# Attention with a routed mixture of experts on one core: weighed values turned by transposing transfers instead of by TensorE

## The chip, the cores and the metric

The kernel runs on one core of one Trainium2 chip. The time is the device time of one launch in microseconds. TensorE (PE) multiplies and transposes through PSUM, VectorE (DVE), ScalarE (ACT) and GpSimd (POOL) work on SBUF and PSUM, and each of them works through its own queue of instructions in order. Transfers are issued by an engine's queue (here mostly SyncE, called SP, and GpSimd) and are carried out by 16 DMA engines.

## What is computed

16 sequences of 256 tokens of width 256, float32. The result is x + attention(layernorm(x)) + experts(layernorm(x)).

```python
# attention: H = 16 heads of hd = 16
q = q * cos + rotate_half(q) * sin              # k likewise
scores = einsum('bhqd,bhkd->bhqk', q, k) / sqrt(16)
attn = softmax(where(causal, scores, lowest))
out = einsum('bhqk,bhkd->bhqd', attn, v)
# experts: E = 8, inner width I = 512
probs = softmax(x @ router_w.T)
w = top_p_weights(probs, 0.9)                   # kept probabilities, not renormalised
for e in range(8):
    out = out + (silu(x @ gate_w[e].T) * (x @ up_w[e].T)) @ down_w[e].T * w[:, e:e+1]
```

## The kernel before

**Tiles.** The 4096 tokens are 32 tiles of 128 (`xs`, resident in SBUF), two to a sequence. The 16 heads are four groups (`c`) of four heads. In PSUM there are two small buffers (`ps_m`) and three of two banks each (`ps_sc`).

**Attention stage (L772 to L900).** For each sequence there are eight steps, two (`p`) to a group of heads, so 128 steps. What a step does, in the order of the code:

- `products` (L657): scores with queries in the partitions (`s`) of this step, and scores with keys in the partitions (`st`) of the step 11 before (`LAG`). The two come in one burst of eight matmuls. Each takes one of the three `ps_sc` buffers.
- `probabilities`: masks added to `st` by matmuls (L694), then one exponential on ScalarE (L699, `pr`), which frees the buffer.
- `maxima` (L670): four VectorE reductions over `s`. They free its buffer. The maxima of a sequence (`top`) are transposed once per sequence by TensorE (`turn`, L682), copied by ScalarE and added to `qT` by GpSimd (L688), so that `st` comes out with its maximum already taken away.
- one job of `prep_jobs` for the next sequence: projections `pq` and `pv` (L525, L541) with their bias additions on VectorE (L530, L545), the copy of the router's `logits` (L551), the rotation of queries and keys (VectorE L560, L561, L563; GpSimd L564, L567), transposes of normalised rows, keys and queries (`xnt` L514, `kt` and `qt` L578), norms on ScalarE (L490), and stores of normalised rows as split 16-bit halves (`half`, L501, stored by SP at L504).
- two steps after every second `st`, `weigh` (L709): eight matmuls multiply the probabilities of four heads with their values and, in a 17th column, with ones. `o` is 128 rows (32 for each head) by 256 tokens. ScalarE copies it to SBUF (`oT`, L715).
- one step later, `finish`: TensorE transposes `oT` back (`ot`, L721, two matmuls into a small PSUM buffer), VectorE takes the reciprocals of the sums (`rs`, L724) and scales (`at`, L726), GpSimd adds to `xs` (L730). After a sequence's last group its two tiles of `xs` are stored to `out`, by SP's queue for the first 13 sequences and by GpSimd's for the last three (L736).
- every second sequence the router (L595 to L626), in pieces over steps: softmax, the comparison of each probability with the others, the kept weights `wts`, stored by SP (L626).

When the last step of `s` is made, the 11 `st` left are made two in a step. The code is written in the order of the program; a scheduler then decides the order in each engine's queue, within what `issue_after` and priorities demand.

**Dispatch.** `count` and `find_wave` (from L257) find, for each expert and each of its rows, which token belongs there. A wave covers up to three blocks of 128 rows for four experts. `fetch` gathers such rows (normalised row and weights) with an indirect DMA of GpSimd (L411).

**Expert stage (L903 to the end).** A list of items: for each expert four groups of up to three blocks. The last item (expert number `E`) is the overflow item of one block, for an expert that more than 1472 tokens chose. For each item: rows gathered two items ahead, turned by `turn_in` one item ahead (a transposing transfer of 16-bit halves on SP, L916, then a copy by VectorE or ScalarE that joins them, L922), `expand` (gate and up products L936, Silu L941, product L942), and one item later `contract`: the product with the third weight (L978), scaling on ScalarE (L985), and an indirect DMA of GpSimd that adds the rows to `out` (L1004). Before the overflow item GpSimd drains its queue (L1036). Waves 2 and 3 of the first four experts are searched in items 0 and 1 (L1015); an item that searches fetches its rows after that.

At the end stands a branch for an expert with more rows than the overflow item holds; it isn't taken.

Of the kernel before, what the change touches and what calls it, by code (L numbers as in the profile page):

```python
# [36 lines left out]
def kernel(  # L37
# [35 lines left out]
    xs = const.tile([P, NT, D], F32, name="xs")  # L73
    nc.sync.dma_start(xs[:, 0:2, :], xf[:, 0:2, :])

    wqkv_sb = const.tile([P, DC, 3 * D + E], F32, name="wqkv_sb")
    nc.sync.dma_start(wqkv_sb[:, :, : 3 * D], wqkv.rearrange("(c p) e -> p c e", p=P))
    nc.sync.dma_start(wqkv_sb[:, :, 3 * D :], wr.rearrange("(c p) e -> p c e", p=P))
# [3 lines left out]
    nc.sync.dma_start(rope_sb, rope.rearrange("(q p) t d -> p q t d", p=P))  # L82
    for t0, t1 in ((2, 4), (4, 8), (8, 16), (16, 24), (24, 32)):
        nc.sync.dma_start(xs[:, t0:t1, :], xf[:, t0:t1, :])
# [236 lines left out]
    def find(h, js, to, numbers, token, name, pool, tag):  # L321
# [4 lines left out]
        def judge(r):  # L326
            nc.vector.tensor_copy(part[:, r, :n, 0:2], seen[r][:, :n, P:])
            for i, j in enumerate(js):
                less = gat.tile([P, P], F32, tag="less", name=f"less_{name}", bufs=2)
# [112 lines left out]
    for e in range(E):  # L442
        work += [(e, js) for js in (GROUPS[-1:] + GROUPS[:-1] if e % 2 else GROUPS)]
    work += [(E, (NB - 1,))]
    AHEAD = 2
    fetched = {}

    with tc.tile_pool(name="prep", bufs=2) as prep, tc.tile_pool(
# [58 lines left out]

        def prep_xnT(b):

            xnT = seqs[b][3]  # L510
            tp = ps_m.tile([P, NQ, DC, P], F32, tag="m", name=f"xnt_{b}")
# [3 lines left out]
            ins = nc.scalar.copy(xnT.rearrange("p c (q t) -> p q c t", q=NQ), tp)  # L515
            if b < 2:
                scalar_last.append(ins.ins)
# [17 lines left out]
        def prep_v(b, qi):  # L535

            t = b * NQ + qi
            xnT = seqs[b][3]
            pv = ps_m.tile([P, D + E], F32, tag="m", name=f"pv_{t}")
            for c in range(DC):  # L540
                nc.tensor.matmul(  # L541
                    pv, xnT[:, c, ts(qi, P)], wqkv_sb[:, c, 2 * D :],
                    start=(c == 0), stop=(c == DC - 1),
                )
            nc.vector.tensor_tensor(  # L545
                va[b % 4][:, qi, :, :HD],
                pv[:, :D].rearrange("p (h d) -> p h d", h=H),
                bias[:, 2 * D :].rearrange("p (h d) -> p h d", h=H),
                ALU.add,
            )  # L550
            nc.vector.tensor_copy(logits[:, t, :], pv[:, D:])  # L551

# [75 lines left out]
        W = 3 * P  # L628

        def products(kinds):  # L630

# [11 lines left out]
            for first in (True, False):  # L643
                for left, right, c, p, sc, by_key in made:
                    if by_key:
                        to, lhs = (slice(2 * P, W), slice(P, S)) if first else (
                            slice(0, 2 * P), slice(0, P))
                    else:
                        to, lhs = (slice(0, P),) * 2 if first else (slice(P, W), slice(P, S))
                    for j in range(2):  # L650
                        rows = slice(32 * (2 * p + j), 32 * (2 * p + j) + 32)

                        with ExitStack() as hold:
                            if opened is not None:
                                hold.enter_context(tc.high_priority(offset=400))
                                hold.enter_context(tc.issue_after(opened.ins))
                            opened = nc.tensor.matmul(  # L657
                                sc[:, j, to], left[rows, c, lhs],
                                right[rows, c, lhs if first else slice(0, S)],
                                start=first, stop=False, skip_group_check=True,  # L660
                            )
            return [m[4] for m in made]

        def maxima(b, c, p, sc):

            for j in range(2):
                for qi in range(NQ):
                    lo, hi = (0, P) if qi == 0 else (P, W)
                    junk = probs.tile([P, 2 * P], F32, tag="junk", name=f"junk_{b}", bufs=2)
                    ins = nc.vector.tensor_tensor_reduce(  # L670
# [6 lines left out]
        def turn(b):  # L677
# [7 lines left out]
            topT = probs.tile([P, S], F32, tag="topT", name=f"topT_{b}", bufs=2)  # L685
            nc.scalar.copy(topT, tp.rearrange("p q t -> p (q t)"))  # L686
# [3 lines left out]
        def probabilities(b, c, p, sc):  # L690

            for j in range(2):
                for k in (0, 2):
# [3 lines left out]
                    )  # L697
            pr = probs.tile([P, 2, W], F32, tag="pr", name=f"pr_{b}_{c}_{p}", bufs=6)
            scalar_last.append(nc.scalar.activation(pr, sc[:, :, :W], AF.Exp).ins)  # L699
            return pr  # L700

        def weigh(b, c, prs):
# [3 lines left out]
            for kc in range(NQ):  # L706
                for hh in range(4):
                    pr, j = prs[hh // 2], hh % 2
                    nc.tensor.matmul(  # L709
                        o[32 * hh : 32 * hh + 32, kc * P :], v[:, kc, 4 * c + hh, :],  # L710
                        pr[:, j, : 2 * P] if kc == 0 else pr[:, j, 2 * P :],
                        start=(kc == 0), stop=(kc == NQ - 1), skip_group_check=True,
                    )
            oT = probs.tile([P, S], F32, tag="oT", name=f"oT_{b}_{c}", bufs=2)
            nc.scalar.copy(oT, o)  # L715
            return oT

        def finish(b, c, oT):
            ot = ps_m.tile([P, NQ, P], F32, tag="m", name=f"ot_{b}_{c}")
            for qi in range(NQ):  # L720
                nc.tensor.transpose(ot[:, qi, :], oT[:, ts(qi, P)], ident)  # L721
            ot = ot.rearrange("p q (h d) -> p (q h) d", d=HP)
            rs = probs.tile([P, NQ * 4], F32, tag="rs", name=f"rs_{b}_{c}", bufs=2)
# [9 lines left out]
            if c == CH - 1:  # L733
                tiles = slice(b * NQ, (b + 1) * NQ)

                queue = nc.sync if b < B - 3 else nc.gpsimd  # L736
                queue.dma_start(of[:, tiles, :], xs[:, tiles, :])
            return ins.ins
# [89 lines left out]
        while late < len(steps) or weighed or finished:  # L828
# [73 lines left out]

    with tc.tile_pool(name="hid", bufs=2) as hid:  # L903

        def open_in(k):
            return hid.tile([P, DC, 3 * P], F32, tag="xT", name=f"xT_{k}")

        turned = {}

        def turn_in(xT, i, xg, name, p0=0, p1=P, pair=None):  # L910
# [3 lines left out]
            if p0 == 0:  # L914
                half = hid.tile([P, 2 * DC, P], U16, tag="half", name=f"xt_{name}_{i}", bufs=6)
# [6 lines left out]
            (nc.scalar.copy if i % 2 else nc.vector.tensor_copy)(  # L922
                both[:, :, :, i * P : i * P + n],
# [90 lines left out]

        waves = {0: [(0, 2)], 1: [(0, 3)]}  # L1015
        for w in range(len(WAVES) - 1):
# [4 lines left out]

        with tc.issue_after(freed[-3]), tc.issue_after(scalar_last[-1]):
            for q in range(len(work[0][1])):
                turn_in(xT[0], q, fetched[0][q][0], 0)
        for i in range(len(work) + 1):
# [14 lines left out]
            if i == 2 * len(GROUPS) - 1:  # L1040
                at_once(count(1))
            searched = chain(*(find_wave(*wave, ps_sc, "sc") for wave in waves.get(i, ())))
            if i == 3 * len(GROUPS) + 2:
# [103 lines left out]
```

## Time and profile before

| | us |
|---|---|
| median of 3 runs | 901.17 (900.65 to 902.33) |
| the profiled execution | 904.55 |
| its span, first to last instruction | 902.8 |
| mean granted TensorE clock in it | 0.991 |

The profile is of one execution. In the table below each row is a group of instructions of one line: how many, their busy time in all and the mean of one.

| line, engine | what | count | busy us | mean ns |
|---|---|---|---|---|
| L936, L978 PE | products of the experts | 1792 | 537.8 | 380 to 481 |
| L657 PE | scores, both kinds | 2048 | 239.2 | 348 and 355 |
| L670 DVE | maxima | 512 | 151.7 | 351 |
| L699 ACT | exponentials | 128 | 103.5 | 811 |
| L1004 POOL | adding rows to `out` | 96 | 150.8 | 1571 |
| L411 POOL | gathering rows | 92 | 97.0 | 1054 |

Matmuls are pipelined, so that the busy times of a group's instructions overlap; how long something holds TensorE is read from start to start. The span in 40 equal slices, with the busy share of each slice in tenths (9 is 90% or more), shows the two stages:

```profile
DVE  3898888878787879743121245432121212111210
ACT  2476565556555555442222222222222222222221
```

VectorE and ScalarE are used heavily in the attention stage, the first 17 slices or so, and lightly in the expert stage.

### The profile page before, as it was taken

The numbers are of one execution on the slowest core, as the hardware profiler recorded it, in microseconds if no ns is written. First come the engines' busy times: TensorE is split into PE (matmuls) and PEld (weight loads), VectorE is DVE, ScalarE is ACT, GpSimd is POOL, SyncE is SP. The second block draws the span as 40 slices with busy tenths as digits, with TensorE's granted clock in tenths as the row PEclk, the third lists the DMA queues.
The fourth block names the chain that finished last, engine by engine and source line by source line (L and its number), as shares of the span: only waits on it lengthen the run. The fifth ranks groups of instructions, "written<-read, shape, count | busy, mean of one in ns | idle before, by whom it ended". The sixth has DMA issues, their size and how long they took to land. (4 is left out here: it accounts for less than half of the span.)

```text
span 902.8 us, 17259 instructions
## 1 busy us (share of the span) xinstructions
PE 875.5 (97%) x6394; PEld 587.8 (65%) x6394; DVE 442.3 (49%) x2067; ACT 349.3 (39%) x644; POOL 404.4 (45%) x475
## 2 busy tenths in 40 slices
PE   7999999999999999989999999999999999999995
PEld 4556666666666666646676666766667766667674
DVE  3898888878787879743121245432121212111210
ACT  2476565556555555442222222222222222222221
POOL 6334333333333332424555545545554464556433
PEclk9999999999999999999999999999999999999998
DMA  7107100000000020134775463565665655656332
GB/s 240 36 8 244 31 25 26 25 26 26 25 26 26 25 95 20 32 78 80 116 134 96 74 146 65 95 103 107 116 103 82 123 99 114 108 82 121 54 36 33
DMA packets 96573, 69.98 MB, mean 78 GB/s; under 512 B 59840, under 2 KB 87616, under 8 KB 96480
## 3 DMA queue, kind: packets, MB, share of 16 engines
q0 software_dynamic: 19792, 30.86, 20.9%
q1 hardware_dynamic: 76688, 37.94, 16.5%
q8 instruction: 52, 0.85, 0.4%
q14 instruction: 41, 0.34, 0.1%
HBM read 32.14 MB, written 24.43 MB: 63 GB/s over the span
## 5 line engine op out<-in xcount | busy, mean ns | idle before, releaser
L1004 POOL DMA_INDIRECT out<-ys,tokens x96 | 150.8, 1571 | 205.4 <-ACT ys L985 188.3
L942 DVE TENSOR_TENSOR hT<-act,gu 128x384 f32<-128x384 f32 (+2 forms) x132 | 69.4, 526 | 258.0 <-ACT act L941 257.8
L936 PE MATMUL gu<-xT,wg 128*128 128x384 f32 (+1 forms) x512 | 183.6, 481 | 3.7 <-ACT oT L715 2.9
L936 PE MATMUL gu<-xT,wu 128*128 128x384 f32 (+1 forms) x512 | 179.8, 474 | 0.0
L978 PE MATMUL py<-wd,hT 128*128 128x256 f32 (+1 forms) x768 | 174.4, 380 | 1.9 <-DVE hT L942 1.9
L978 PEld LDWEIGHTS py<-wd,hT 128*128 128x128 f32 (+1 forms) x768 | 137.7, 186 | 40.2 <-DVE hT L942 2.3
L670 DVE CUSTOM_DVE_ANT_0 junk<-s,mask 128x128 f32<-128x128 f32 (+1 forms) x512 | 151.7, 351 | 17.2 <-PE s L657 15.9
L941 ACT ACTIVATE act<-gu 128x384 f32<-128x384 f32 (+2 forms) x132 | 62.2, 471 | 243.1 <-PE gu L936 243.1
L699 ACT ACTIVATE pr<-st 128x768 f32<-128x768 f32 x128 | 103.5, 811 | 102.2 <-PE st L694 100.0
L936 PEld LDWEIGHTS gu<-xT,wu 128*128 128x128 f32 x512 | 97.9, 191 | 61.9 <-issue 1.7
L936 PEld LDWEIGHTS gu<-xT,wg 128*128 128x128 f32 x512 | 96.7, 192 | 48.9 <-ACT oT L715 3.2
L657 PE MATMUL st<-qT,kT 32*128 32x128 f32 (+1 forms) x1024 | 120.6, 355 | 0.5 <-POOL qT L688 0.5
L657 PE MATMUL s<-kT,qT 32*128 32x128 f32 (+1 forms) x1024 | 118.6, 348 | 2.1 <-ACT pr L699 1.3
L411 POOL DMA_INDIRECT xg<-rows,tokens x92 | 97.0, 1054 | 37.3 <-issue 25.9
L730 POOL TENSOR_TENSOR xs<-xs,at 128x128 f32<-128x128 f32 x64 | 30.1, 471 | 140.2 <-DVE at L726 139.0
L985 ACT ACTIVATE ys<-py,xg 128x256 f32<-128x256 f32 (+1 forms) x96 | 45.4, 473 | 115.8 <-PE py L978 114.4
L657 PEld LDWEIGHTS st<-qT,kT 32*128 32x128 f32 x1024 | 68.7, 184 | 22.1 <-issue 16.9
L922 DVE COPY xT<-xt 128x512 uint16<-128x512 uint16 x65 | 25.9, 442 | 99.7 <-PE gu L936 84.5
L657 PEld LDWEIGHTS s<-kT,qT 32*128 32x128 f32 x1024 | 67.4, 185 | 7.2 <-issue 3.0
L525 PE MATMUL pq<-wqkv_sb,xnT 128*128 128x512 f32 x128 | 63.8, 622 | 3.6 <-DVE qk L530 2.2
L688 POOL TENSOR_TENSOR qT<-qT,topT 128x256 f32<-128x256 f32 x64 | 50.8, 826 | 22.2 <-ACT topT L686 22.2
L564 POOL TENSOR_TENSOR kp<-qk,rot 128x256 f32<-128x256 f32 x32 | 23.2, 726 | 77.3 <-DVE rs L724 42.5
(162 smaller groups left out, 942.3 us busy)
## 6 DMA issues: line engine op xcount, KB each, us to landing
rows<-half SPq DMA_DIRECT2D x32, 128.0 KB, 1.7
wg<-in_wg SPq DMA_DIRECT2D x8, 512.0 KB, 4.0
wu<-in_wu SPq DMA_DIRECT2D x8, 512.0 KB, 6.3
wd<-in_wd SPq DMA_DIRECT2D x8, 512.0 KB, 3.9
out<-xs SPq DMA_DIRECT2D x13, 256.0 KB, 2.2
xs<-in_x SPq DMA_DIRECT2D x3, 1024.0 KB, 11.6
rows<-zeros POOLq DMA_DIRECT2D x1, 1716.0 KB, 8.7
out<-zeros POOLq DMA_DIRECT2D x1, 1664.0 KB, 13.3
```

The lines of the kernel that those rows point to most:

```text
L411: nc.gpsimd.indirect_dma_start(out=xg[:n, :], out_offset=None, in_=halves, in_offset=bass.IndirectOffsetOnAxis(ap=token, axis=0),)
L525: nc.tensor.matmul(pq, xnT[:, c, ts(qi, P)], wqkv_sb[:, c, : 2 * D], start=(c == 0), stop=(c == DC - 1),)
L657: opened = nc.tensor.matmul(sc[:, j, to], left[rows, c, lhs], right[rows, c, lhs if first else slice(0, S)], start=first, stop=False, skip ...
L670: ins = nc.vector.tensor_tensor_reduce(junk[:, : hi - lo], sc[:, j, lo:hi], mask[:, 2 * P - (hi - lo) :], -1.0, -MASKED, ALU.add, ALU.min, ...
L688: nc.gpsimd.tensor_tensor(qT[:, c, :], qT[:, c, :], topT, ALU.add)
L699: scalar_last.append(nc.scalar.activation(pr, sc[:, :, :W], AF.Exp).ins)
L936: nc.tensor.matmul(gu[:, j, :w], w_sb[:, c, ts(i, P)], xT[:, c, :w], start=(c == 0), stop=(c == DC - 1),)
L941: nc.scalar.activation(act[:, :w], gu[:, 0, :w], AF.Silu)
L942: nc.vector.tensor_tensor(hT[:, i, :w], act[:, :w], gu[:, 1, :w], ALU.mult)
L978: nc.tensor.matmul(py[p0:p1, :], hT[:, i, k * P : k * P + p1 - p0], expert_w[e][2][:, i, :], start=(i == 0), stop=(i == IC - 1), skip_grou ...
L985: nc.scalar.activation(ys[p0:p1, :], py[p0:p1, :], AF.Copy, scale=weights_of(e, xg, p0, p1))
L1004: ins = nc.gpsimd.indirect_dma_start(out=out, out_offset=bass.IndirectOffsetOnAxis(ap=to[:p1, :], axis=0), in_=ys[:p1, :], in_offset=None, ...
```

## The change

The main part is in `weigh` and `finish`. ScalarE now copies `o` to SBUF as two planes of 16-bit halves (the low and the high halves of each float32 number). A transposing transfer in SP's queue turns these 512 rows of 128 halves into `half`. GpSimd joins the halves to float32 numbers in SBUF (`ot`, 17 of each 32 columns). VectorE's reciprocal and its multiplication then read SBUF where they read PSUM before. TensorE no longer takes part, and no small PSUM buffer is used. In the code `finish` stands four steps after the weighing instead of one (two in the tail).

```diff
-            oT = probs.tile([P, S], F32, tag="oT", name=f"oT_{b}_{c}", bufs=2)
-            nc.scalar.copy(oT, o)
-            return oT
+            tensor_last.append(ins.ins)
+            oT = probs.tile([P, 2, S], U16, tag="oT", name=f"oT_{b}_{c}", bufs=3)
+            nc.scalar.copy(oT, o.bitcast(U16).rearrange("p (s h) -> p h s", h=2))
+            half = probs.tile([P, 2, NQ * 4, HP], U16, tag="oh", name=f"oh_{b}_{c}", bufs=3)
+            nc.sync.dma_start_transpose(
+                half.rearrange("p h (q g) d -> p (h q) (g d)", q=NQ),
+                oT.rearrange("p h s -> p (h s)"),
+            )
+            return half
...
-            ot = ps_m.tile([P, NQ, P], F32, tag="m", name=f"ot_{b}_{c}")
-            for qi in range(NQ):
-                nc.tensor.transpose(ot[:, qi, :], oT[:, ts(qi, P)], ident)
-            ot = ot.rearrange("p q (h d) -> p (q h) d", d=HP)
+            ot = probs.tile([P, NQ * 4, HD + 2], F32, tag="ot", name=f"ot_{b}_{c}", bufs=2)
+            both = ot.rearrange("p g d -> p (g d)").bitcast(U16)
+            both = both.rearrange("p (g d h) -> p h g d", g=NQ * 4, h=2)
+            nc.gpsimd.tensor_copy(both[:, :, :, : HD + 1], half[:, :, :, : HD + 1])
             rs = probs.tile([P, NQ * 4], F32, tag="rs", name=f"rs_{b}_{c}", bufs=2)
             nc.vector.reciprocal(rs, ot[:, :, HD])
...
-                queue = nc.sync if b < B - 3 else nc.gpsimd
-                queue.dma_start(of[:, tiles, :], xs[:, tiles, :])
+                nc.gpsimd.dma_start(of[:, tiles, :], xs[:, tiles, :])
...
-                    finished.setdefault(i + 3, []).append(k)
+                    finished.setdefault(i + (6 if i < len(steps) else 4), []).append(k)
```

All stores of rows to `out` are thereby issued by GpSimd. The other edits:

**Tail of the attention stage.** Where two `st` are made in a step, their burst may only be issued behind the last weighing so far.

```diff
+                            elif len(kinds) == 2 and kinds[1][1] and tensor_last:
+                                hold.enter_context(tc.issue_after(tensor_last[-1]))
```

**Buffers.** `less`, `junk` and `topT` have one buffer instead of two, `pr` five instead of six.

**Start.** The first two tiles of `xs` come in a transfer each. Of `wqkv` only the columns of queries and keys come ahead of the bias and the rotation's factors; those of the values and of the router come behind. The statistics, norms and transposes of sequence 0 are made tile by tile. Those of tiles 2 and 3 come behind the last `logits` copy of sequence 0.

```diff
-        for t in range(NQ):
-            sums_of(t)
-        statistics(0, NQ)
...
-        prep_norm(0)
-        prep_xnT(0)
-        for t in range(NQ, 2 * NQ):
-            sums_of(t)
-        statistics(NQ, NQ)
+        for qi in range(NQ):
+            sums_of(qi)
+            statistics(qi, 1)
+            prep_norm(0, (qi,))
+            prep_xnT(0, qi, 1)
         for qi in range(NQ):
             prep_qk(0, qi)
-            prep_v(0, qi)
+            ins = prep_v(0, qi)
             for _ in rotation():
                 pass
+        with tc.issue_after(ins.ins):
+            for t in range(NQ, 2 * NQ):
+                sums_of(t)
+            statistics(NQ, NQ)
```

**Into the experts.** The first three `turn_in` stand behind the fourth last addition to `xs` alone (before: behind the third last and the last exponential), their buffers come from a pool of their own (`rows_in`), and their copies are all made by VectorE. Both waves are searched in item 0, one before each of its second and third quarters.

```diff
-        waves = {0: [(0, 2)], 1: [(0, 3)]}
+        waves = {0: [(0, 2), (0, 3)]}
...
-        with tc.issue_after(freed[-3]), tc.issue_after(scalar_last[-1]):
+        with tc.issue_after(freed[-4]):
...
-                if q == 1 and i in waves:
-                    at_once(searched)
-                    if i + AHEAD < len(work):
+                if q > 0 and searches:
+                    at_once(searches.pop(0))
+                    if q == 1 and i + AHEAD < len(work):
                         fetched[i + AHEAD] = fetch(*work[i + AHEAD])
```

**End.** The overflow item stands ahead of the last item instead of behind it.

```diff
-    work += [(E, (NB - 1,))]
+    work.insert(len(work) - 1, (E, (NB - 1,)))
```

More of the change, by code (lines that the diff above doesn't have):

```diff
@@ L73 @@
     xs = const.tile([P, NT, D], F32, name="xs")
-    nc.sync.dma_start(xs[:, 0:2, :], xf[:, 0:2, :])
+    for t in range(2):
+        nc.sync.dma_start(xs[:, t : t + 1, :], xf[:, t : t + 1, :])
     wqkv_sb = const.tile([P, DC, 3 * D + E], F32, name="wqkv_sb")
-    nc.sync.dma_start(wqkv_sb[:, :, : 3 * D], wqkv.rearrange("(c p) e -> p c e", p=P))
-    nc.sync.dma_start(wqkv_sb[:, :, 3 * D :], wr.rearrange("(c p) e -> p c e", p=P))
+    wf = wqkv.rearrange("(c p) e -> p c e", p=P)
+    nc.sync.dma_start(wqkv_sb[:, :, : 2 * D], wf[:, :, : 2 * D])
     bias = const.tile([P, 3 * D], F32, name="bias")
@@ L82 @@
     nc.sync.dma_start(rope_sb, rope.rearrange("(q p) t d -> p q t d", p=P))
+    nc.sync.dma_start(wqkv_sb[:, :, 2 * D : 3 * D], wf[:, :, 2 * D :])
+    nc.sync.dma_start(wqkv_sb[:, :, 3 * D :], wr.rearrange("(c p) e -> p c e", p=P))
     for t0, t1 in ((2, 4), (4, 8), (8, 16), (16, 24), (24, 32)):
@@ L328, in judge @@
             for i, j in enumerate(js):
-                less = gat.tile([P, P], F32, tag="less", name=f"less_{name}", bufs=2)
+                less = gat.tile([P, P], F32, tag="less", name=f"less_{name}", bufs=1)
                 nc.vector.tensor_scalar(
@@ L506, in store, with prep_xnT @@
             )
-        def prep_xnT(b):
+        def prep_xnT(b, q0=0, n=NQ):
             xnT = seqs[b][3]
-            tp = ps_m.tile([P, NQ, DC, P], F32, tag="m", name=f"xnt_{b}")
+            tp = ps_m.tile([P, n, DC, P], F32, tag="m", name=f"xnt_{b}_{q0}")
             for qi, xn in enumerate(normed.pop(b)):
@@ L514, in prep_xnT @@
                     nc.tensor.transpose(tp[:, qi, c, :], xn[:, ts(c, P)], ident)
-            ins = nc.scalar.copy(xnT.rearrange("p c (q t) -> p q c t", q=NQ), tp)
+            ins = nc.scalar.copy(
+                xnT.rearrange("p c (q t) -> p q c t", q=NQ)[:, q0 : q0 + n], tp
+            )
             if b < 2:
@@ L550, in prep_v @@
             )
-            nc.vector.tensor_copy(logits[:, t, :], pv[:, D:])
+            return nc.vector.tensor_copy(logits[:, t, :], pv[:, D:])
         def rotation():
@@ L628 @@
         W = 3 * P
+        tensor_last = []
         def products(kinds):
@@ L668, in maxima @@
                     lo, hi = (0, P) if qi == 0 else (P, W)
-                    junk = probs.tile([P, 2 * P], F32, tag="junk", name=f"junk_{b}", bufs=2)
+                    junk = probs.tile([P, 2 * P], F32, tag="junk", name=f"junk_{b}", bufs=1)
                     ins = nc.vector.tensor_tensor_reduce(
@@ L684, in turn @@
                 )
-            topT = probs.tile([P, S], F32, tag="topT", name=f"topT_{b}", bufs=2)
+            topT = probs.tile([P, S], F32, tag="topT", name=f"topT_{b}", bufs=1)
             nc.scalar.copy(topT, tp.rearrange("p q t -> p (q t)"))
@@ L697, in probabilities @@
                     )
-            pr = probs.tile([P, 2, W], F32, tag="pr", name=f"pr_{b}_{c}_{p}", bufs=6)
+            pr = probs.tile([P, 2, W], F32, tag="pr", name=f"pr_{b}_{c}_{p}", bufs=5)
             scalar_last.append(nc.scalar.activation(pr, sc[:, :, :W], AF.Exp).ins)
@@ L708, in weigh @@
                     pr, j = prs[hh // 2], hh % 2
-                    nc.tensor.matmul(
+                    ins = nc.tensor.matmul(
                         o[32 * hh : 32 * hh + 32, kc * P :], v[:, kc, 4 * c + hh, :],
@@ L713, in weigh, with finish @@
                     )
-            oT = probs.tile([P, S], F32, tag="oT", name=f"oT_{b}_{c}", bufs=2)
-            nc.scalar.copy(oT, o)
-            return oT
-        def finish(b, c, oT):
-            ot = ps_m.tile([P, NQ, P], F32, tag="m", name=f"ot_{b}_{c}")
-            for qi in range(NQ):
-                nc.tensor.transpose(ot[:, qi, :], oT[:, ts(qi, P)], ident)
-            ot = ot.rearrange("p q (h d) -> p (q h) d", d=HP)
+            tensor_last.append(ins.ins)
[5 more added lines that the diff above has]
+                oT.rearrange("p h s -> p (h s)"),
+            )
+            return half
+        def finish(b, c, half):
+            ot = probs.tile([P, NQ * 4, HD + 2], F32, tag="ot", name=f"ot_{b}_{c}", bufs=2)
+            both = ot.rearrange("p g d -> p (g d)").bitcast(U16)
+            both = both.rearrange("p (g d h) -> p h g d", g=NQ * 4, h=2)
+            nc.gpsimd.tensor_copy(both[:, :, :, : HD + 1], half[:, :, :, : HD + 1])
             rs = probs.tile([P, NQ * 4], F32, tag="rs", name=f"rs_{b}_{c}", bufs=2)
@@ L900 @@
         at_once(todo)
-    with tc.tile_pool(name="hid", bufs=2) as hid:
+    with tc.tile_pool(name="rows_in", bufs=2) as rows_in, tc.tile_pool(
+        name="hid", bufs=2
+    ) as hid:
         def open_in(k):
-            return hid.tile([P, DC, 3 * P], F32, tag="xT", name=f"xT_{k}")
+            return rows_in.tile([P, DC, 3 * P], F32, tag="xT", name=f"xT_{k}")
         turned = {}
@@ L914, in turn_in @@
             if p0 == 0:
-                half = hid.tile([P, 2 * DC, P], U16, tag="half", name=f"xt_{name}_{i}", bufs=6)
+                half = rows_in.tile(
+                    [P, 2 * DC, P], U16, tag="half", name=f"xt_{name}_{i}", bufs=6
+                )
                 nc.sync.dma_start_transpose(half, xg[:, : 2 * D])
@@ L921, in turn_in @@
             both = both.rearrange("p (c t h) -> p h c t", c=DC, h=2)
-            (nc.scalar.copy if i % 2 else nc.vector.tensor_copy)(
+            (nc.scalar.copy if i % 2 and name else nc.vector.tensor_copy)(
                 both[:, :, :, i * P : i * P + n],
@@ L1041 @@
                 at_once(count(1))
-            searched = chain(*(find_wave(*wave, ps_sc, "sc") for wave in waves.get(i, ())))
+            searches = [find_wave(*wave, ps_sc, "sc") for wave in waves.get(i, ())]
             if i == 3 * len(GROUPS) + 2:
```

## The prediction, made before the changed kernel ran

> **What bounds it now.** First the busy shares and the table of stretches: in the attention stage (46 to 393 us of the span) and in the expert stage TensorE never rests for long, so what it does and what makes it wait is the time. Columns of the second fence: stretch, then length and busy time of TensorE, its weight loads, VectorE, ScalarE, GpSimd, then TensorE's granted clock and the DMA share.
>
> ```profile
> PE 875.5 (97%) x6394; PEld 587.8 (65%) x6394; DVE 442.3 (49%) x2067; ACT 349.3 (39%) x644; POOL 404.4 (45%) x475
> ```
> ```profile
> 84.00:107.00 23.00, 22.68 (x272) 14.30 (x271) 21.33 (x108) 14.82 (x27) 8.14 (x12) 1.00 0.36 114
> ...
> 199.00:222.00 23.00, 23.00 (x278) 14.82 (x276) 19.32 (x98) 15.86 (x28) 7.89 (x12) 1.00 0.07 23
> 222.00:245.00 23.00, 23.00 (x291) 14.75 (x294) 18.26 (x92) 12.88 (x24) 8.31 (x13) 1.00 0.09 27
> ```
>
> One sequence (eight steps) lasts 22.45 us: `top` is turned every 22.45 us in the steady part. TensorE is full there, but VectorE is at 79 to 84%: the second bound is close, and it works strictly in its queue's order. Next the order of TensorE's instructions in time:
>
> ```profile
> 205.60 0.86 PE L709 MATMUL o<-pr,va 128*32 128x256 f32 x16
> 206.39 0.38 PE L657 MATMUL st<-qT,kT 32*128 32x128 f32 x2
> ...
> 207.49 0.61 PE L578 MATMUL kt<-ident,kp 128*128 128x128 f32 x4
> 207.93 0.38 PE L721 MATMUL ot<-ident,oT 128*128 128x128 f32 x2
> 208.25 0.49 PE L657 MATMUL st<-qT,kT 32*128 32x128 f32 x4
> ```
>
> From start to start, `ot` (L721) holds TensorE for 0.32 us, a weighing 0.79, and by the same reading a burst of scores 0.87, its masks 0.23, `kt` or `qt` 0.44, `xnt` 0.53, `top` 0.32, `pq` 1.77, `pv` 1.04.
>
> **What is taken away.** 64 pairs of `ot`, 0.32 us each: 20 us if nothing takes their place. They cover something, though: before the burst at 208.25 ScalarE's exponential must have freed a score buffer, and of the 1.28 us per sequence some 0.3 would return as that wait. Net 1.0 us per sequence, 14 us in all. VectorE's own work hardly changes.
>
> **What takes its place.** The weighed values now go ScalarE, SP's queue, a transposing transfer, GpSimd's copy, VectorE's reciprocal. Built up from rows, from the end of a weighing to the start of its reciprocal:
> - to ScalarE's copy 0.19 (206.39 to 206.58 in the trace);
> - the copy, now 512 halves: 0.60 (the same split at L501 takes 0.61, 512 numbers out of PSUM at L580 0.58; the old copy 0.37);
> - to SP 0.1;
> - issue and landing 2.4;
> - to GpSimd 0.1, its copy of 272 halves 0.5, to VectorE 0.1.
>
> The transfer's rows:
> ```profile
> rows<-half SPq DMA_DIRECT2D x32, 128.0 KB, 1.7
> ...
> xt<-xg SPq DMA_TRANSPOSE x92, 3.2
> ```
> "Advanced Engine Details and Errata" of the Trainium skill, X-Bar Transpose (TRN2), says that transposing transfers are as fast as regular ones. That would be 1.7 us, the plain store of 128 KB. The row of the expert stage's transfers of the same size says 3.2, least 2.3, of which SP's issue alone is 1.19. I take 2.4, near the least, since the DMA share is 0.08 in the attention stage and about 0.55 in the expert stage. GpSimd's copy has no row: a fill of 256 takes 0.30 and an addition of 128 numbers 0.46, of 256 numbers 0.73; so 0.3 to 0.8, and 0.5 as it has one input. Sum: **L = 4.0 us**, from 3.3 (rule) to 5.1.
>
> The title's four steps would be some 11 us, enough for any of these. But the built order does not keep them. In VectorE's queue each reciprocal stands where the scheduler thought its input ready: in the steady part two of the four of a sequence come after the first two maxima of the next burst, two after the last maxima of the burst before the weighing, with only a `qk` bias or a multiplication between. None is four steps away. So VectorE, and with it the maxima behind the reciprocal, waits for the chain; and the maxima free the score buffers.
>
> I walked one sequence through the queues at L = 4.0. Third weighing's end is 0. Reciprocal at 4.0; it, the two maxima left and the scaling, 1.0; the `qk` multiplication 0.61; the router's part at this place 1.75 (products 0.64, reduction 0.42, two of 0.3, and gaps); four maxima 1.2. Only now, at 8.55, has the buffer for the second burst after the next weighing come free; TensorE would be there at about 6.3. From that burst to the next third weighing TensorE needs 14.78: four more bursts and masks with what stands between them, in the slots above. In it lies one more wait: the first weighing's reciprocal, then scaling, maxima, `va`, rotation and `logits` (2.9) hold a PSUM buffer of the second `pq`: 4.0 + 2.9 against 6.35 that TensorE needs, 0.55. Sum 8.55 + 14.78 + 0.55 = **23.9, against 22.45: 1.43 us more** per sequence. At 3.3 it would be 22.6, no change; at 5.1 it would be 26.1.
>
> **SP's queue** adds to it. In six of the eight sequences whose router ends, its store of `wts` stands just before the fourth transfer, and that store waits for VectorE, which is now late: `wts` at 7.36, store 0.4, transfer 2.4, copy and steps 0.7, and 1.0 of work behind the reciprocal: 11.9, where TensorE would need the buffer at 10.6. About 1.4 us, six times.
>
> Counting twelve sequences in full (two early ones are bound by VectorE already: 21.33 of 23 us in the first row above): 12 x 1.43 + 6 x 1.4 = **25.6 us slower**.
>
> **GpSimd and the shared port.** Per sequence it gets four copies (2.0) and one store (0.75, from L737) on 8 of 22.45 us: no bound. All 16 stores of rows cost 0.75 us of its queue each; only additions that nobody needs soon stand behind. "SBUF — State Buffer", two separate sides, says that a VectorE operation with two SBUF inputs blocks against a GpSimd operation that reads SBUF. The scaling read PSUM until now (always 0.29); after the change both inputs are in SBUF. The row is L563, of that kind: 0.69, but 1.11 beside the `qT` additions.
> ```profile
> 201.60 1.11 DVE L563 TENSOR_TENSOR qk<-qk,rope_sb 128x512 f32<-128x512 f32 x1
> ```
> By the rule each scaling could lose up to 0.7, 2.9 per sequence. By the rows one in four does, and L560 and L561 (mean 426 and 417) lose next to nothing: 0 to 0.4, which I leave at nothing in the sum.
>
> **The smaller edits.**
> - Start: the bias lands earlier (9.4 now, with 256 KB less ahead), so the first `qk` moves from 12.36 to about 9. But the statistics of tiles 2 and 3 now stand behind the second `logits`, and TensorE's order puts their `xnt` and `pq` before the first `kt`: kt0 at 20.7 now, 20.5 to 23 after. +1 (from -2 to +2.5).
> - Tied double bursts: they give up nothing, as the exponentials pace them; five `ot` less, -1.5.
> - Into the experts: now TensorE idles 2.95 us at 393 since ScalarE waits for a transfer before copying `oT`, and the second expert matmul group starts 9 us after the last weighing. After: the last transfer lands some 4 us after it, copy, scaling and addition follow, and the first Silu waits for that addition; about 8. But late tokens hold SP's queue, with the last four transfers behind: +1 (-1 to +5).
> - Both searches in the first item: about 2.2 us more idle there; in return the gathers for the fourth item start earlier, and the stall of 1.9 us at 432 with the slower clock behind it (0.83 in that stretch) goes: -1.2.
> - End: the overflow item is now last but one.
> ```profile
> 893.09 0.47 ACT L985 ACTIVATE ys<-py,weight 128x256 f32<-128x256 f32 x1 [1.45 <-PE py L978]
> 897.50 1.55 POOL L1004 DMA_INDIRECT out<-ys,rows_f  x1 [4.72 <-ACTq L1066]
> ```
> The last scatter starts 4.4 us after the last matmul (893.05), held by the drain. After, three scatters 1.85 us apart end the kernel, the last starting 1.7 after it: -2.75.
> - One buffer fewer for `junk`, `less`, `topT`, `pr`: maxima that wait for their own engine already follow without a gap (0.00 in the trace): 0.
>
> Sum: 25.6 + 1 - 1.5 + 1 - 1.2 - 2.75 = **+22**. The profiled execution is 904.55 (span 902.8), so 926.7; the median lies 3.4 below it: **923**.
>
> **Rivals.**
> - *The wait stays hidden* (0.19): landing and copy are quicker than I think, or VectorE has the slack. Then 14 us of `ot` less and 4.5 of the rest: 883. For it: VectorE idles some 3 us per sequence. Against it: 2.3 is the least transfer seen, and break-even needs L of about 3.3.
> - *A draw near break-even* (0.15): L 3.3 to 3.6, 898 to 912; 0.03 of it lies within 0.2%, 0.12 above.
> - *The transfer as slow as in the expert stage* (0.16): landing 3.2, copy 0.76, L 5.1: 3.65 a sequence, 12 x 3.65 + 8 - 3.5 = +48, 949.
> - *The forecast* (0.50): 912 to 938.
>
> The range 886 to 950 leaves out most of the first rival's lower half and the end of the third. Faster by over 0.2% (about what a measurement of this kernel can tell from no change) 0.19, within it 0.03, slower 0.78.
>
> **What would show it.** VectorE's reciprocals waiting for GpSimd's `ot` copies, some 1 to 3 us each; TensorE waiting at bursts for VectorE's maxima, 1 to 2 us per sequence, `top` every 24 us and not 21.5; transfers landing in about 2.4 us; the store of `wts` late on SP. Wrong if `top` comes every 21.5 us, or if TensorE waits for something else, such as ScalarE.

## The result: 12% slower, five times the loss that was forecast

The changed kernel takes 1015.66 us (median of 4 runs, 1007.88 to 1019.91), the kernel before 901.75 beside it: ratio 1.1233, 95% interval 1.1193 to 1.1273. Forecast were 923 us and a range of 886 to 950. The profiled execution has a span of 1010.1 us against 902.8. All of the loss lies ahead of the experts' first product, which starts at 506.98 us instead of 395.64; from there to the last matmul it is 495.8 us instead of 497.4.

First the busy shares and the slices of the page after the change.

```profile
PE 911.5 (90%) x6266; PEld 598.0 (59%) x6266; DVE 486.4 (48%) x2070; ACT 364.8 (36%) x645; POOL 445.8 (44%) x552
...
DVE  3885777787777767765261222534321111121110
...
PEclk8998898999999999977689999999999999999999
```

The attention stage now reaches into slice 21. TensorE's share has gone from 97% to 90%, and its granted clock is lower (0.942 on average against 0.991). VectorE has *more* busy time than before, 486.4 against 442.3 us, though the same operations are left to it. That was not in the sum.

The table of stretches of the changed kernel (stretch, length, busy time of TensorE, its weight loads, VectorE, ScalarE, GpSimd, then granted clock, DMA share, GB/s):

```profile
84.00:107.00 23.00, 15.23 (x139) 9.65 (x138) 13.04 (x62) 10.04 (x16) 7.83 (x12) 0.78 0.89 239
...
199.00:222.00 23.00, 20.62 (x238) 13.10 (x236) 18.74 (x88) 11.61 (x21) 7.73 (x14) 0.93 0.16 41
222.00:245.00 23.00, 20.15 (x225) 12.21 (x223) 17.65 (x80) 11.87 (x19) 8.42 (x14) 0.93 0.19 44
```

In the steady part TensorE pauses 2.4 to 2.9 us of 23, and the row at 84 is far worse: 7.8 us of pauses beside a DMA share of 0.89. Last, the chain of waits for one weighing (start, us, what):

```profile
199.75 0.83 PE o L720 x16
...
200.61 0.59 ACT oT L728
...
201.26 2.43 DMA oh<-oT
...
203.81 0.52 POOL ot L740
204.35 0.20 DVE rs L742
204.55 0.16 DVE junk L681
204.72 0.21 DVE at L744
204.93 0.33 DVE junk L681
205.27 0.74 DVE qk L569
...
206.14 0.73 DVE r_p L604
206.89 0.02 ACT r_p L605
...
207.03 0.80 ACT pr L710
...
207.88 0.38 PE s L668 x2
```

From the weighing over ScalarE, the transfer, GpSimd, VectorE and ScalarE again back to a burst of scores: every engine waits for the one before it. The links are as forecast (copy 0.59, landing 2.43, GpSimd's copy 0.52), and from the weighing's end to the reciprocal it is 3.8 us. But the reciprocal and the scaling stand *between* maxima (`junk`) of one burst. The end of this chain is a path that the prediction didn't have: the router's exponential (`r_p`) waits for a late VectorE and holds up the exponential behind it in ScalarE's queue (`pr`), which frees a score buffer.

What TensorE and ScalarE waited for from 107 to 500 us (engine, line, what it waited for: us in all, times, longest):

```profile
PE st L668 <- DVE top L681: 20.3, 19, 2.5
PE s L668 <- ACT pr L710: 13.2, 8, 2.1
PE pq L531 <- DVE logits L557: 12.1, 11, 2.0
```
```profile
ACT r_p L605 <- DVE r_p L604: 24.2, 6, 4.4
```

In the list before the change (90 to 420 us) none of TensorE's three waits appears, and ScalarE's is 6.9. The first and the third are the two that the prediction walked through: bursts that wait for maxima, some 1.5 us per sequence, and `pq` for the buffer that `logits` frees. The second is one that it named as a sign of being wrong, ScalarE; where the chain above passes, it is VectorE's delay handed on.

### The profile page after: what moved, and what is told of

Same layout as the page of the kernel before. It is cut to its first block, busy times and chain, and to the rows that moved or that the text cites. A ratio compares the mean times of both kernels' runs of the same rounds, so it can differ in the third digit from the quotient of the medians.

```text
span 1010.1 us, 17190 instructions
## 1 busy us (share of the span) xinstructions
PE 911.5 (90%) x6266; PEld 598.0 (59%) x6266; DVE 486.4 (48%) x2070; ACT 364.8 (36%) x645; POOL 445.8 (44%) x552
## 4 chain that ended last, share of the span: by engine, by line
PE 67%; DVE 13%; DMA 10%; ACT 3%; issue 3%; POOL 3%; SPq 0%; POOLq 0%; ACTq 0%; DVEq 0%
PE gu L958 32%; PE py L1000 16%; DMA oh<-oT 10%; DVE junk L681 5%; PE st L668 4%; PE pq L531 3%; PE o L720 3%; PE s L668 2%; PE pv L547 2%; ACT oT L728 2%; POOL ot L740 2%; PE st L705 2%; DVE rot L567 1%; DVE qk L569 1%; ACT pr L710 1%
## 5 line engine op out<-in xcount | busy, mean ns | idle before, releaser
L681 DVE CUSTOM_DVE_ANT_0 junk<-s,mask 128x128 f32<-128x128 f32 (+1 forms) x512 | 179.8, 351 | 20.4 <-PE s L668 7.7
L668 PE MATMUL st<-qT,kT 32*128 32x128 f32 (+1 forms) x1024 | 143.2, 402 | 23.8 <-DVE top L681 22.4
L668 PE MATMUL s<-kT,qT 32*128 32x128 f32 (+1 forms) x1024 | 133.8, 382 | 23.1 <-ACT pr L710 13.2
L668 PEld LDWEIGHTS st<-qT,kT 32*128 32x128 f32 x1024 | 79.4, 211 | 65.6 <-DVE top L681 37.8
L740 POOL COPY ot<-oh 128x272 uint16<-128x272 uint16 x64 | 32.8, 515 | 189.0 <-DMA oh<-oT 188.8
L668 PEld LDWEIGHTS s<-kT,qT 32*128 32x128 f32 x1024 | 75.5, 205 | 33.7 <-ACT pr L710 18.2
L944 DVE COPY xT<-xt 128x512 uint16<-128x512 uint16 (+1 forms) x66 | 26.3, 449 | 91.0 <-PE gu L958 88.5
L720 PE MATMUL o<-pr,va 128*32 128x256 f32 (+1 forms) x1024 | 61.9, 354 | 0.8 <-ACT oT L728 0.6
L742 DVE RECIPROCAL rs<-ot 128x8 f32<-128x8 f32 x64 | 13.0, 203 | 98.1 <-POOL ot L740 94.5
```

The costliest lines, as they stand in the source:

```text
L668: opened = nc.tensor.matmul(sc[:, j, to], left[rows, c, lhs], right[rows, c, lhs if first else slice(0, S)], start=first, stop=False, skip ...
L681: ins = nc.vector.tensor_tensor_reduce(junk[:, : hi - lo], sc[:, j, lo:hi], mask[:, 2 * P - (hi - lo) :], -1.0, -MASKED, ALU.add, ALU.min, ...
L720: ins = nc.tensor.matmul(o[32 * hh : 32 * hh + 32, kc * P :], v[:, kc, 4 * c + hh, :], pr[:, j, : 2 * P] if kc == 0 else pr[:, j, 2 * P :] ...
L740: nc.gpsimd.tensor_copy(both[:, :, :, : HD + 1], half[:, :, :, : HD + 1])
```

## The experiments

Three theories at first. **A**: the reciprocals stand too early in VectorE's queue. **B**: the way over four queues slows the engines wherever they stand. **C**: the smaller edits and the fewer buffers cost the time. The ratios are to the kernel before.

**The reciprocals really late (e1).**

```diff
-                vector_last = finish(steps[k][0], steps[k][1], held.pop(k))
+                with tc.issue_after(behind.ins):
+                    vector_last = finish(steps[k][0], steps[k][1], held.pop(k))
```

> The changed kernel with one edit: everything in finish is issued behind the maxima of the step in which it stands in the code, so that in VectorE's built order the reciprocal comes 3 to 4 bursts after its weighing (0 to 1 in the changed kernel). Theory A (the place of the reciprocals in VectorE's queue makes each transfer's way a wait that TensorE sees): the waits of rs for ot, 94 us in 58 places, go nearly to nothing, a sequence lasts 21 to 22.5 us as before the change, and the time is 885 to 915. Theory B (the way itself, over ScalarE, SP, GpSimd and the shared port, slows the engines wherever the reciprocal stands): still above 960. Theory C (the smaller edits and buffers cost it): still above 960.

935.88 us, ratio 1.0374 (1.0318 to 1.0430), between what A expected and what B and C did. 80 us come back, but not the rest. The row of the reciprocals says that the waits of A are nearly gone (busy us, mean ns, then idle time before them with what ended it):

```profile
L742 DVE RECIPROCAL rs<-ot 128x8 f32<-128x8 f32 x64 | 12.3, 192 | 19.4 <-POOL ot L740 17.6 <-issue 1.8
```

19.4 us of waiting. In the page of the changed kernel the same row has 98.1:

```profile
L742 DVE RECIPROCAL rs<-ot 128x8 f32<-128x8 f32 x64 | 13.0, 203 | 98.1 <-POOL ot L740 94.5
```

So the place of the reciprocals in the queue makes most of the loss, and something else costs some 30 us.

**TensorE's transposes back, all other edits kept (e2)**: `weigh` and `finish` as before, one step apart.

> The changed kernel with TensorE's transposes back (weigh and finish as before, one step apart), all other edits kept, GpSimd's stores and the fewer buffers among them. Theories A and B: 890 to 905, near the kernel before, the end 2 to 3 us better and the start 1 to 4 worse. Theory C: above 930.

927.19 us, ratio 1.0257 (1.0210 to 1.0304). Just under what C expected, and far above A and B: the smaller edits cost 24.4 us (927.19 against 902.76) without any transposing transfer.

**Only the transfers, and the buffers that make room for them (e3)**: the kernel before with the `weigh` and `finish` of the change.

> The kernel before with only the transposing transfers (weigh and finish of the change, at the changed steps) and the fewer buffers that they need to fit; start, tail, entry, waves, end as before, row stores of the first 13 sequences on SP again. Theories A and B: 1000 to 1025, as the changed kernel. Theory C: below 980.

1016.17 us, ratio 1.1224 (1.1143 to 1.1305), the whole loss again, without the new start, tail, waves and end. What e2 and e3 share is the fewer buffers. Among them is `junk`, the output of the maxima that nobody reads, on the engine whose busy time grew. That is theory **D**.

**One buffer of `junk` alone, in the kernel before (e4).**

```diff
-                    junk = probs.tile([P, 2 * P], F32, tag="junk", name=f"junk_{b}", bufs=2)
+                    junk = probs.tile([P, 2 * P], F32, tag="junk", name=f"junk_{b}", bufs=1)
```

> The kernel before with one buffer of junk instead of two, nothing else. Theory D (with one buffer each maximum waits for the end of the one before it, though both stand on VectorE; its busy time in the attention stage grows by 28 us, from 82% to 91% of the steady part): VectorE's group of maxima 152 to 180 us busy, the time 3 to 12 us up. Rival (the prediction's step: maxima on one engine follow each other anyway): the same time within 2 us.

925.44 us, ratio 1.0250 (1.0211 to 1.0290): 22 us for one word. The timeline of VectorE, first before the change with two buffers (start, us, engine, line, what):

```profile
210.04 0.28 DVE L670 CUSTOM_DVE_ANT_0 junk<-s,mask 128x128 f32<-128x128 f32 x1
210.25 0.08 DVE L670 DVE_READ_ACCUMULATOR2_ANT top<- 128x1 f32 x1
210.25 0.41 DVE L670 CUSTOM_DVE_ANT_0 junk<-s,mask 128x256 f32<-128x256 f32 x1
210.60 0.08 DVE L670 DVE_READ_ACCUMULATOR2_ANT top<- 128x1 f32 x1
210.60 0.28 DVE L670 CUSTOM_DVE_ANT_0 junk<-s,mask 128x128 f32<-128x128 f32 x1
```

and with one buffer (e4):

```profile
210.03 0.42 DVE L670 CUSTOM_DVE_ANT_0 junk<-s,mask 128x256 f32<-128x256 f32 x1
210.38 0.08 DVE L670 DVE_READ_ACCUMULATOR2_ANT top<- 128x1 f32 x1
210.50 0.29 DVE L670 CUSTOM_DVE_ANT_0 junk<-s,mask 128x128 f32<-128x128 f32 x1
210.72 0.08 DVE L670 DVE_READ_ACCUMULATOR2_ANT top<- 128x1 f32 x1
210.83 0.42 DVE L670 CUSTOM_DVE_ANT_0 junk<-s,mask 128x256 f32<-128x256 f32 x1
```

With two buffers a maximum starts together with the reading of the accumulator before it (210.25 and 210.25), so it overlaps the end of the maximum before (210.04 + 0.28). With one it starts 0.12 us later (210.38 to 210.50). The group of maxima in e4:

```profile
L670 DVE CUSTOM_DVE_ANT_0 junk<-s,mask 128x128 f32<-128x128 f32 (+1 forms) x512 | 181.3, 354 | 19.7 <-PE s L657 8.1
```

It is busy 181.3 us instead of 151.7, at nearly the same mean (354 and 351 ns): the mean doesn't show it, the busy sum, in which overlaps count once, does.

**Two buffers of `junk` in e2 (e5) and in the changed kernel (e6).**

> TensorE's transposes with the other edits of the change, but two buffers of junk. Theory D: a sequence 22.2 us again instead of 22.3 to 23.3, 912 to 920; what is left above the kernel before is the start, which at the second turn of maxima was 15 us late. Rival (the maxima cost nothing, the start all of it): 925 to 930.

> The changed kernel with two buffers of junk. If VectorE is what the sequence of waits runs through, 1.7 us of its time per sequence come back in full: 980 to 995. If the reciprocals' waits take up what it gains: 1005 to 1020.

e5: 903.69 us, ratio 1.0019 (1.0000 to 1.0037); of e2's 24.4 us 23.5 were the one buffer, more than expected. The other fewer buffers (`less`, `topT`, `pr`) are still in e5 and cost nothing there that can be told. e6: 967.19 us, ratio 1.0691 (1.0632 to 1.0750): 48.5 us off the changed kernel. So the buffer costs twice as much there. And yet the reciprocals wait nearly as long in e6 as in the changed kernel (98.1):

```profile
L742 DVE RECIPROCAL rs<-ot 128x8 f32<-128x8 f32 x64 | 13.0, 202 | 93.2 <-POOL ot L740 90.2
```

The sum of these waits is thus not the loss; what stands behind a waiting reciprocal counts, as e13 shows below. So e1's 80 us and these 48.5 overlap: a late reciprocal doesn't stand between maxima either.

**Late reciprocals, two buffers, the start as before (e7).**

> The kernel with the late reciprocals, two buffers of junk, and the start as in the kernel before. If the transposing transfers are worth what they take from TensorE once VectorE neither waits nor is full: 21.0 to 21.6 us per sequence, 885 to 900. If VectorE or GpSimd's shared port is the bound in their place: 22.2 and more per sequence, 905 to 920.

914.95 us, ratio 1.0141 (1.0093 to 1.0190), as the second of its two expectations has it. A sequence lasts 22.02 us in the mean of eight (from turn to turn of `top`, sequences 4 to 12), against 22.23 in the kernel before: hardly a gain, though TensorE has 1.25 us less to do. Where that went, summed from start to start of TensorE's groups over the same eight sequences, us per sequence:

| | scores | `pq` | masks | `kt` | `ot` | all others |
|---|---|---|---|---|---|---|
| before | 7.72 | 3.54 | 1.87 | 0.89 | 1.25 | 6.96 |
| e7 | 8.32 | 3.73 | 1.93 | 1.08 | 0 | 6.95 |

1.04 of the 1.25 us come back as longer slots of what follows, 0.60 of it at the bursts of scores. Either the transposes had stood in waits for a score buffer or for operands that are there without them too, or the new work makes operands late (the rotation's two products on VectorE take 523 and 589 ns in e7 instead of 426 and 417). No run here tells the two apart.

**The loads and fills of the third sequence moved away (e8).** Expert 0's weights and both zero fills go from steps 20 and 24 to step 2, in e6.

> The changed kernel with two buffers of junk, in which the loads of expert 0 and both zero fills (4.9 MB together) are issued behind the maxima of step 2, before any weighing, instead of in steps 20 and 24. If the third sequence's 41 us (24 before the change) come from transposing transfers that land 7 to 12 us late beside these loads: the third sequence 25 to 27 us, and 950 to 955 instead of 967. If they come from the order of VectorE's queue there: 963 to 970.

956.83 us against 967.19, and the third sequence lasts 32.6 us instead of 41.2, not the 25 to 27 expected; the loads and fills explain some 10 us, not all of that sequence. (The two intervals overlap, 1.0551 to 1.0657 against 1.0632 to 1.0750, so that the sequence's 8.5 us in the traces are the better figure.) What they do, in e6: the rows of three stretches, then GpSimd's and SP's timelines (in brackets the idle time before it, and for what).

```profile
82.00:90.00 8.00, 4.34 (x60) 2.74 (x52) 4.22 (x20) 1.33 (x3) 2.19 (x4) 0.90 1.03 229
90.00:98.00 8.00, 6.97 (x68) 4.98 (x72) 5.89 (x34) 5.22 (x10) 3.01 (x3) 0.67 0.80 231
98.00:106.00 8.00, 3.14 (x28) 1.42 (x20) 1.48 (x7) 4.49 (x6) 1.13 (x3) 0.97 1.02 256
```
```profile
103.92 0.50 POOL L740 COPY ot<-oh 128x272 uint16<-128x272 uint16 x1 [10.75 <-DMA oh<-oT]
```
```profile
92.00 9.95 SPq L730 DMA_TRANSPOSE oh<-oT  x2
```

The transfer issued at 92.00 (the first of the two in that row) is there for GpSimd at 103.92: 11.9 us instead of 2.5, at a DMA share of 0.80 to 1.02.

**The store of `wts` by GpSimd (e9)**, in e6.

> The changed kernel with two buffers of junk and the store of wts issued by GpSimd, so that no transposing transfer waits behind it on SP. The prediction's step (1.4 us in each of six sequences): 957 to 961 instead of 967. Rival (the wait only moves, to GpSimd's copies or to VectorE): 965 to 970.

961.28 us against 967.19: 5.9 us, of the 8.4 that the prediction had for it. That is not clear of noise: the four runs of e6 go from 959.62 to 969.36, those of e9 from 957.89 to 961.49. In the traces a sequence is 0.3 us shorter (23.97 against 24.28).

**A mixture (e10)**: e7 with e8's early loads, and TensorE's transposes for the last two sequences.

> The kernel with late reciprocals, two buffers of junk and the start as before, with the loads of expert 0 and the zero fills behind step 2, and with TensorE's transposes kept for the last two sequences. If the collision of sequence 3 (6 us) and the tail (10 us) are what kept e7 at 915: 895 to 900, 0.3 to 0.8% faster than the kernel before. If the late reciprocals cost elsewhere: 905 to 912.

908.41 us, ratio 1.0050 (1.0031 to 1.0069). 6.5 us better than e7, where the hopeful one of two expectations had 15 to 20, and still slower than the kernel before: a sequence lasts 22.03 us, and from the last turn of `top` to the experts' first product it is 28.9 us (25.1 before the change), also with TensorE's transposes there. But the third sequence lasts 24.1 us, as before the change: with late reciprocals and early loads nothing of its delay is left.

**What is left without the transfers (e11)**: e5 with the start as before.

> TensorE's transposes, two buffers of junk and the start as before: what is left of the change is the tail, the way into the experts, the waves, the end and GpSimd's stores. By the prediction's terms without the start (-1.2 for the waves, -2.75 for the end, 0 to +1 for the entry): 898 to 901. If the entry and the waves cost what the end brings: 902 to 905.

898.69 us, ratio 0.9955 (0.9931 to 0.9979): the one version here that beats the kernel before. Against e5 (903.69) it puts the new start at 5.0 us of loss.

**Order or time between maxima (e12, e13).** One buffer has two effects. Beside the 0.12 us, other work of VectorE comes to stand in the gap when the scheduler orders the queue: of the gaps between the four maxima of a burst, in the built order, 8 hold such an instruction in the kernel before, 83 in e4, 109 in the changed kernel (28 reciprocals and 27 scalings among them) and 6 in e6. e12 is e4 with reciprocals, `va` and `logits` issued behind the burst's maxima. e13 is the changed kernel with reciprocals and `va` so placed; the reciprocals stand nearly all where e6 has them.

```diff
-            nc.vector.reciprocal(rs, ot[:, :, HD])
+            with behind_maxima(...):
+                nc.vector.reciprocal(rs, ot[:, :, HD])
```

> The kernel before with one buffer of junk, in which reciprocals, the additions for va and the logits copies are issued behind all four maxima of the step (with one buffer, 83 of the gaps between the maxima of a burst hold such an instruction in the built order; with two, 8; here 12). If the single buffer's 22 us come from this order, which frees the score buffer later: 903 to 910. If they come from the 0.11 us between two maxima that write the same buffer: 920 to 926.

> The changed kernel, still with one buffer of junk, in which the reciprocals and the additions for va are issued behind all four maxima of a burst, at the places that they have with two buffers (in the changed kernel 55 reciprocals and scalings and 30 additions stand between the maxima of one burst). If the single buffer costs 48 us here since VectorE waits for a transfer with the burst's maxima still to do, and so holds its score buffer: 970 to 985. If it is the 0.11 us between maxima, taken from an engine that has no slack: 1000 to 1016.

e12: 929.69 us, ratio 1.0289 (1.0240 to 1.0338), no better than e4, and per sequence (mean of eight) 22.81 us against 22.72 in e4 and 22.23 with two buffers: in the kernel before it is the time between maxima. (What the forced order costs by itself, with two buffers, no run shows.) e13: 991.30 us, ratio 1.1000 (1.0975 to 1.1025), in the middle between both expectations. So of the 48.5 us in the changed kernel 24.4 are the order (1015.66 to 991.30) and 24.1 the time between maxima (991.30 to 967.19). Per sequence it is 27.51, 25.82 and 24.28 us, so half and half again. This second half, 1.5 us per sequence, is three times what it is in the kernel before (0.5, e4); why wasn't tested. The order costs something only where a reciprocal waits for a transfer. In the changed kernel's timeline:

```profile
210.25 0.42 DVE L681 CUSTOM_DVE_ANT_0 junk<-s,mask 128x256 f32<-128x256 f32 x1
210.59 0.08 DVE L681 DVE_READ_ACCUMULATOR2_ANT top<- 128x1 f32 x1
...
211.39 0.51 POOL L740 COPY ot<-oh 128x272 uint16<-128x272 uint16 x1 [3.90 <-DMA oh<-oT]
...
211.93 0.20 DVE L742 RECIPROCAL rs<-ot 128x8 f32<-128x8 f32 x1 [1.26 <-POOL ot L740]
...
212.05 0.24 DVE L681 CUSTOM_DVE_ANT_0 junk<-s,mask 128x128 f32<-128x128 f32 x1
...
212.43 0.42 DVE L681 CUSTOM_DVE_ANT_0 junk<-s,mask 128x256 f32<-128x256 f32 x1
```

Two maxima of the burst are done at 210.67. VectorE then stands still for 1.26 us until GpSimd's copy is done, with the other two maxima behind, and with them the score buffer that a later burst of TensorE needs.

## Why the prediction was wrong

The direction and the main mechanism were right; the size was off by a factor of five (+22 forecast, +114 measured), and the step that failed first is this one: "One buffer fewer for `junk`, `less`, `topT`, `pr`: maxima that wait for their own engine already follow without a gap (0.00 in the trace): 0." It cost 48.5 us (e6). A gap of 0.00 was read as "waiting costs nothing", while the records showed an overlap of 0.07 us that a wait takes away. And no term held what else one buffer does: it lets the scheduler put reciprocals between maxima, which is half of the 48.5 (e13). The Trainium skill points the same way as that step ("VectorE: DVE Perf Modes", The DRAIN you can't avoid): copies with a semaphore after each were as fast as with one after the last. Those were plain copies; for these reductions the measurement decides: from the start of a maximum to that of the next it is 0.33 us for 128 columns and 0.47 for 256 where both write one buffer, against 0.21 and 0.35 (the rows of e4 and of the kernel before above).

Point by point:

- **Way of a weighing, L = 4.0.** Right in its links, and the shortest are 3.7 to 3.8. Over the steady part of the changed kernel (44 weighings) the median is 4.8, since at two of the four places of a sequence something stands ahead on a queue: at the second GpSimd's copy starts 4.3 us after the issue instead of 2.5, right behind the rotation's products, and at the fourth, in every second sequence, the store of `wts` is ahead on SP and the issue 2.3 to 3.1 us late. The prediction gave GpSimd 0.1. By its own slope (23.9 at 4.0, 26.1 at 5.1) 4.8 would be some 25.5 us per sequence, an estimate.
- **The walk through a sequence.** The number came out near, in part by luck. The walk took two buffers' times for the maxima, but the order of one buffer (reciprocals behind the first two maxima of a burst). No run has that pair. In e6, with two buffers and no reciprocal between maxima, a sequence lasts 24.28 us; in e9, without the store of `wts` on SP, 23.97. Forecast were 24.6 with the store in every second sequence and 23.9 without. But a sequence of the kernel before lasts 22.23 in the mean of eight; 22.45 is the longest of them. So e9 adds 1.74, where 1.43 were forecast. With the order that the walk took it would be more: that order costs 1.69 with one buffer (27.51 in the changed kernel, 25.82 in e13).
- **`wts` on SP, 1.4 us six times.** 5.9 of 8.4 us (e9), within the noise of e6's runs.
- **`ot` taken away, 0.3 of 1.28 us per sequence back as waits.** Mis-sized: 1.04 of 1.25 came back (e7), from waits uncovered or from new ones. So the rival "the wait stays hidden" at 883 was not to be had: with late reciprocals and two buffers it is 915.
- **The transfer's 2.4 us.** Right by itself (2.43), but taken for every transfer. Beside loads and fills it was 11.9, and these cost some 10 us (e8). The prediction knew the 512 KB loads and the fills from their rows and didn't set them against the new transfers; of the 3.2 us transfers that it took its figure from, the longest landed after 8.2.
- **Start, +1.** 5.0 (e5 against e11).
- **Tied bursts in the tail, -1.5.** The last three intervals between turns of `top` sum to 71.3 us in e6, 60.1 before the change. The tied bursts are not the cause: e5 has them too, with TensorE's transposes, and takes 60.7. With late reciprocals (e7) it is 61.2.
- **Into the experts, +1.** Mis-sized: from the last turn of `top` to the experts' first product e6 takes 35.8 us, the kernel before 25.1. In the tail nothing is left to stand between weighing and reciprocal, and VectorE waits 5 to 6 us at some of them. With late reciprocals (e7) it is still 35.0.
- **Waves, -1.2, and end, -2.75.** As forecast: 1.6 us less from the first product to the last matmul, and from there to the end 7.3 us instead of 9.75. In the changed kernel the last scatter follows soon:

```profile
997.32 5.49 PE L1000 MATMUL py<-wd,hT 128*128 128x256 f32 x24
```
```profile
1003.86 1.55 POOL L1026 DMA_INDIRECT out<-ys,tokens  x1 [0.31 <-issue]
```

- **GpSimd's shared port, left at 0.** In the changed kernel the scalings were hardly slower (295 ns, 292 before), in e6 353. There 15 of the 64 overlap an addition or copy of GpSimd; 13 of these take 352 to 861 ns, and the 49 others at most 294. In the kernel before, where the scaling reads PSUM, 27 overlap such work and all take 291 or 292. The rule that the prediction cites from the Trainium skill ("SBUF — State Buffer", SBUF: two separate sides), that a VectorE operation with two SBUF inputs blocks against a GpSimd operation that reads SBUF, agrees with these figures. The rotation's two products grew as well: 555 and 648 ns against 426 and 417, 11.5 us of VectorE in all. But this is not the new copies' doing. Of the 26 products that took over 480 ns, 25 overlap the old additions to `qT`, and none overlaps a copy; in e4, without any such copy, the second product takes 636. What moved is when they meet.

The account, then. Of the 114 us, 48.5 are the one buffer. What is left can be laid out from two profiles, e6 beside the kernel before (965.6 and 902.8 us), in us: first turn of `top` 4.5 later, third sequence 17.0, last three intervals 11.2, the other eleven 22.7, way from the last turn to the experts' first product 10.7, from there to the end -3.3; in all 62.8. Some of these have a cause shown by a run: the start 5.0 (e5 against e11), the loads and fills 8.5 of the 17.0 (e8), the reciprocals' place most of the last three (e7) and, with the loads, the third sequence (e10).

Not settled: which wait keeps the third sequence of e8 at 32.6 us, why the way into the experts stays long in e7 and e10, and what the lower clock (0.942) costs by itself. TensorE's clock is lower in several stretches with pauses or just behind one (0.78 and 0.93 in the rows of the changed kernel, 0.67 in e6 from 90 to 98 us), but not in all (0.97 there from 98 to 106), and no run here holds one of the two fixed.

## What to carry to other kernels

A buffer taken away is an edit with a price, also where its writers stand on one engine: compare the busy sum of the group, not the mean, and look in the built order for what the scheduler now puts between instructions that belonged together. A long way over several queues costs little only if its last instruction stands late in the queue of the engine that waits; the place in the code doesn't put it there. And work taken from the engine that is the bound need not come back as time: here a sixth of it did (0.21 of 1.25 us per sequence, e7).

## What the runs showed of the hardware

- A maximum that writes another buffer than the one before starts with the reading of the accumulator; one that writes the same buffer starts 0.12 us later. Over 512 maxima the busy sum grows by 30 us (151.7 to 181.3), and the kernel by 22 (e4).
- A transposing transfer of 128 KB from SBUF to SBUF lands 2.4 to 2.5 us after its issue at a DMA share of 0.16 to 0.19, and was there 11.9 us after it beside loads and fills (share 0.80 to 1.02, e6). That such transfers are as fast as regular ones, as the prediction cites it from the Trainium skill ("Advanced Engine Details and Errata", X-Bar Transpose (TRN2)), doesn't show at this size: the plain store of 128 KB, from SBUF to HBM, took 1.7.
- A multiplication of VectorE with one input in PSUM took 291 or 292 ns also where it overlapped GpSimd's work (27 scalings, kernel before). With both inputs in SBUF, 13 of the 15 that overlapped it took 352 to 861 ns (e6).
